# One change to a graph-attention front end on one Trainium2 core: source-term row spread ahead of the branch, first head's bounds spread by TensorE, out-degrees tied into the attention, edge test behind the first counts

## The chip, the cores and the metric

The kernel runs on one core of one Trainium2 chip. The metric is device time in microseconds; of a kernel measured several times the median counts. The kernel before took 3251.81, 3253.80 and 3253.83 us in three runs, median 3253.8.

Names of the engines: PE is TensorE's matmul stream and PEld its weight loads, DVE is VectorE, ACT ScalarE, POOL GpSimd, SP SyncE. DMAs are issued by SP and by POOL here.

## The reference

A chain of four residual stages on 1250 nodes of 1024 features with 20,000 directed edges, sorted by destination:

```python
x = x + gat(layernorm(x), W, a_l, a_r, src, dst)      # 4 heads of 256
x = x + rail_ffn(layernorm(x), ...)                    # 16384 hidden, GELU, dense way down
x = x + gcn(layernorm(x), edges, W, b)                 # degree-normalized sums
x = x + moe(layernorm(x), ...)                         # top 1 of 8 GEGLU experts, and a shared one
```

The change lies in the first stage and in one input of the third:

```python
z  = einsum('ni,hif->nhf', h, W)
el = einsum('nhf,hf->nh', z, a_l);  er = einsum('nhf,hf->nh', z, a_r)
e  = leaky_relu(el[src] + er[dst], 0.2)
ex = exp(e - segment_max(e, dst)[dst])
alpha = ex / segment_sum(ex, dst)[dst]
out = segment_sum(alpha * z[src], dst)                 # GAT
deg = 1 + (number of edges that leave a node)          # GCN uses deg ** -0.5
```

## The kernel before

Nodes are worked in T = 10 tiles of R = 125, edges in EC = 160 chunks of 125. The edge lists aren't followed one by one: the kernel builds the dense matrix of edge counts, destination by source, and does the attention densely with the counts as weights.

**Counts.** The edge lists are turned onto partitions as `ef`. For each chunk DVE makes a one-hot of the sources (`os`, 1250 wide) and one of the destinations (`od`, one or two tiles wide), and TensorE multiplies them into `pc`. `count(d)` does so for the chunks in which destination tile d can occur, given that the list is sorted and roughly even (`win[d]`, 19 chunks for the first tile); `finish` copies the counts, writes them to DRAM (`cnt_d`), writes a mask `nm` (0 where there is an edge, -1e30 elsewhere) to `nm_d`, and keeps the transposed counts in `CT` (int16, on chip). An edge test (`lim`, `out_of`, `bad`, `pf`, `flag`, lines 169 to 185) finds out whether any edge lies outside the chunks assumed for it. If so, a branch (`tc.If(elsewhere > 0)`, line 251) counts again over all chunks. With these inputs it isn't taken, but every engine waits at it and meets the others after it.

**Projections.** `z_tile(g, t)` multiplies the normalized nodes of tile t with the weights of heads 2g and 2g+1, copies the product to `Z` (ACT), and DVE forms `el` and `er` for these two heads by four dots (`sc`, line 143). The first pair of heads is projected between the counts, the second after the branch.

**Maxima and bounds.** `el` of two heads is turned into a row, written to DRAM (`to_row`: a TensorE transpose, a copy `st` on ACT, a DMA of POOL) and broadcast from there to 125 partitions (`spread`: another DMA of POOL) as `els`. `maxima(g)` then reads `nm` back tile by tile and takes the maximum of `nm + els` for each destination and head (line 271). It is advanced three steps per `z_tile`. From the maxima `bounds(g)` makes, per head, two values for each destination (`bd`), turns them into a row and spreads it likewise: `rr`, of 2 x 1250 per partition. These rows carry the head's destination term and stabilizer for every partition of the attention.

**Attention.** `attend(h, b)` does head h for half b of the destinations. For each of the ten source tiles s: DVE forms `u` from the row `rr` and per-source terms (line 316), ACT takes the exponential (317), DVE multiplies with the counts (`w`, 320), and TensorE does five matmuls of `w` with `Z` (322), whose last column of ones gives the denominators. At the end DVE divides and adds into `X`, the residual (327 to 330). `u` and `w` have three buffers. The order is attend(0,0), (0,1), (1,0), `bounds(1)`, (1,1), (2,0), (3,0), (2,1), (3,1). The maxima of heads 2 and 3 run between the steps of (0,1) and (1,0). The out-degrees `dis` are ten row sums of `CT` on DVE, then a square root and a reciprocal; they are written beside attend(1,1) but depend on nothing there.

**Order.** A planner puts the instructions of each engine into an order of its own between such constraints; the order in the source is not the order on the engine. `tc.issue_after(x)` makes the planner place an instruction behind x. A pool's memory is handed to the next pool when its last readers are done, and the first writer there waits for them.

Of the kernel before, what the change touches and what calls it, by code (L numbers as in the profile page):

```python
# [8 lines left out]
F32 = mybir.dt.float32  # L9
# [10 lines left out]
P = 128  # L20
# [17 lines left out]
def gnn_ffn_kernel(ctx, tc, x, src, dst, gat_w, a_l, a_r, maker, up, cproj,  # L38
# [64 lines left out]
    nc.gpsimd.memset(Z[:, :, :, F:F + 1], 1.0)  # L103
    el, er, mx, el2, el8 = (zp.tile([R, H, T], F32, name=n) for n in ("el", "er", "mx", "el2", "el8"))
    xT = xTp.tile([P, KD, N], F32, name="xT")

    def to_row(pool, psp, cols, k, n):

# [5 lines left out]
        nc.gpsimd.dma_start(row, st)  # L114
        return row

    def el_row(g, pool, psp):
        return to_row(pool, psp, el[:, 2 * g:2 * g + 2, :].rearrange("p h t -> p (h t)"), 2 * T, f"el{g}")

    def spread(dst_t, row):  # L120

        nc.gpsimd.dma_start(dst_t, row.rearrange("k r -> (k r)").partition_broadcast(R))

    with tc.tile_pool(name="gw", bufs=1) as gwp, tc.tile_pool(name="gps", bufs=3, space=PSUM) as psp:
        W, aw = {}, {}
# [20 lines left out]
        with tc.tile_pool(name="cc", bufs=1) as ccp, tc.tile_pool(name="cw", bufs=2) as cwp:  # L146
# [10 lines left out]
            with tc.tile_pool(name="ce", bufs=1) as cep:  # L157
                ei = cep.tile([EC // 2, 2, 2, EP], I32, name="ei")
                for i, e in enumerate((src, dst)):
                    nc.sync.dma_start(ei[:, i], e.rearrange("(a c p) -> c a p", c=EC // 2, p=EP))  # L160
                eif = cep.tile([EC // 2, 2, 2, EP], F32, name="eif")
                nc.vector.tensor_copy(eif, ei)
                pe = psp.tile([EP, 2, EC], F32, name="pt")
                for i in range(2):
                    for g in range(2):
                        nc.tensor.transpose(pe[:, i, g * EC // 2:(g + 1) * EC // 2], eif[:, i, g, :],
                                            ident[:EC // 2, :EC // 2])
                nc.vector.tensor_copy(ef, pe)
                lim = cep.tile([EP, 2, EC], F32, name="lim")
                c0 = 0  # L170
                for c in range(1, EC + 1):
                    if c == EC or near[c] != near[c0]:
                        nc.gpsimd.memset(lim[:, 0, c0:c], float(near[c0][0] * R))
                        nc.gpsimd.memset(lim[:, 1, c0:c], float((near[c0][-1] + 1) * R))
                        c0 = c
                out_of = cep.tile([EP, 2, EC], F32, name="out_of")
                nc.vector.tensor_tensor(out_of[:, 0], ef[:, 1], lim[:, 0], op=ALU.is_lt)
                nc.vector.tensor_tensor(out_of[:, 1], ef[:, 1], lim[:, 1], op=ALU.is_ge)
                bad = cep.tile([EP, 1], F32, name="bad")
                nc.vector.tensor_reduce(bad, out_of.rearrange("p a c -> p (a c)"), AX.X, ALU.add)  # L180
                ones_col = cep.tile([EP, 1], F32, name="ones_col")
                nc.gpsimd.memset(ones_col, 1.0)
                pf = psp.tile([1, 1], F32, name="pt")
                nc.tensor.matmul(pf, bad, ones_col, start=True, stop=True)
                nc.vector.tensor_scalar(flag, pf, 0.0, None, op0=ALU.is_gt)

            def src_hot(pool, c, bufs):
                os = pool.tile([EP, N], F16, name="os", bufs=bufs)
                nc.vector.tensor_scalar(os, iota, ef[:, 0, c:c + 1], None, op0=ALU.is_equal)
# [23 lines left out]
            with tc.tile_pool(name="hot", bufs=1) as hotp, tc.tile_pool(name="gl", bufs=2) as lnp:  # L213
                hot, norm = {}, {}

                def count(d):
                    pc = psp.tile([R, 3, 512], F32, name="pc", bufs=1)
                    for c in win[d]:
                        if c not in hot:
                            hot[c] = src_hot(hotp, c, 9), dst_hot(hotp, c, near[c], 9)  # L220
                        os, od = hot[c]
                        for b, (n0, nn) in enumerate(NCH):
                            nc.tensor.matmul(pc[:, b, :nn], od[:, d - near[c][0], :], os[:, n0:n0 + nn],  # L223
                                             start=(c == win[d][0]), stop=(c == win[d][-1]))
                    finish(d, pc)

                xt = {}

                def load_x(t):
                    xt[t] = lnp.tile([R, D], F32, name="xt", bufs=4)  # L230
                    dma(nc.sync, xt[t], x_t[t])

                for t in range(4):
                    load_x(t)
                z_weights(0)
                count(0)
                for t in range(T):
                    normalize(norm, lnp, t, xt[t], xt[t])
                    turn(xT, norm, psp, t, 3)
                    z_tile(0, t)  # L240
                    if t + 4 < T:
                        load_x(t + 4)
                    if t % 2:
                        count((t + 1) // 2)
                z_weights(1)
                for d in range(T // 2 + 1, T):
                    count(d)
            row0 = el_row(0, cwp, psp)

            elsewhere = nc.values_load(flag[0:1, 0:1], min_val=0, max_val=1)  # L250
            with tc.If(elsewhere > 0):  # L251
# [7 lines left out]
                                                 start=(c == 0), stop=(c == EC - 1))  # L259
                        finish(d, pc)  # L260

        def maxima(g, mxp, row):

            els = mxp.tile([R, 2, N], F32, name="els")
            spread(els.rearrange("p a n -> p (a n)"), row)
            for d in range(T):
                nm = mxp.tile([R, N], F32, name="nm2", bufs=3 - g)
                dma(nc.sync, nm, nm_d[d])
                for h in (2 * g, 2 * g + 1):
                    sc = mxp.tile([R, N], F32, name="sc2")  # L270
                    nc.vector.tensor_tensor_reduce(sc, nm, els[:, h - 2 * g, :], scale=1.0, scalar=-3.0e38,  # L271
                                                   op0=ALU.add, op1=ALU.max, accum_out=mx[:, h, d:d + 1])
                    yield

        def bounds(g, pool, psp, rowp):

            hs = slice(2 * g, 2 * g + 2)
            for dst_t, f in ((el2, SLOPE), (el8, 1.0 - SLOPE)):
                nc.vector.tensor_scalar(dst_t[:, hs], el[:, hs], f, None, op0=ALU.mult)
            top = pool.tile([R, 2, T], F32, name="top")  # L280
            nc.vector.tensor_tensor(top, mx[:, hs], er[:, hs], op=ALU.add)
            nc.vector.scalar_tensor_tensor(top, top, SLOPE, top, op0=ALU.mult, op1=ALU.max)
            bd = pool.tile([R, 2, 2, T], F32, name="bd")
            nc.vector.tensor_tensor(bd[:, :, 0], er[:, hs], top, op=ALU.subtract)
            nc.vector.scalar_tensor_tensor(bd[:, :, 1], er[:, hs], SLOPE, top, op0=ALU.mult, op1=ALU.subtract)
            for h in range(2):
                rows[2 * g + h] = rowp.tile([R, 2, N], F32, name="rr", bufs=2)
                spread(rows[2 * g + h].rearrange("p a n -> p (a n)"),
                       to_row(pool, psp, bd[:, h].rearrange("p a t -> p (a t)"), 2 * T, f"bd{2 * g + h}"))

# [1 line left out]
        rowst = ExitStack()  # L292
        rowp = rowst.enter_context(tc.tile_pool(name="rowp", bufs=1, side="right"))
        with tc.tile_pool(name="mx0", bufs=1) as mxp:
            search = maxima(0, mxp, row0)
            for t in range(T):
                for _ in range(3):
                    next(search, None)
                z_tile(1, t)
            bounds(0, mxp, psp, rowp)  # L300
# [7 lines left out]
    with tc.tile_pool(name="att", bufs=3) as atp, tc.tile_pool(name="aps", bufs=6, space=PSUM) as aps, \  # L308
            tc.tile_pool(name="tps0", bufs=2, space=PSUM) as tps:

        def attend(h, b, between=iter(())):
# [12 lines left out]
            for i in range(HT):  # L324

                rs = small.tile([R, 1], F32, name="rs")
                nc.vector.tensor_scalar(rs, po[i][:, F:F + 1], 0.5, None, op0=ALU.max)
                nc.vector.reciprocal(rs, rs)
                xs = X[:, b * HT + i, h * F:(h + 1) * F]
                nc.vector.scalar_tensor_tensor(xs, po[i][:, :F], rs, xs, op0=ALU.mult, op1=ALU.add)  # L330

        with tc.tile_pool(name="mx1", bufs=1) as mxp:
            def degrees():

                for t in range(T):
                    nc.vector.tensor_reduce(dis[:, t:t + 1], CT[:, t, :], AX.X, ALU.add)
                    if t == T - 1:
                        nc.vector.tensor_scalar(dis, dis, 1.0, None, op0=ALU.add)
                        nc.scalar.activation(dis, dis, AF.Sqrt)
                        nc.vector.reciprocal(dis, dis)  # L340
                    yield

            row1 = el_row(1, mxp, tps)
            attend(0, 0)
            search = maxima(1, mxp, row1)
            attend(0, 1, search)
            attend(1, 0, search)
            bounds(1, mxp, tps, rowp)
            attend(1, 1, degrees())
        xT = xTp.tile([P, KD, N], F32, name="xT")  # L350
        with tc.tile_pool(name="al", bufs=2) as lnp:
            attend(2, 0)
# [517 lines left out]
```

## Time and profile before

| | value |
|---|---|
| median of 3 runs | 3253.8 us |
| profiled execution | 3250.55 us, its span 3248.8 us |
| TensorE busy | 3156.3 us, 97% of the span |
| DVE / ACT / POOL busy | 51% / 11% / 4% |
| first count matmul | 12.28 us |
| branch left behind | about 246 us |
| first maximum | 261.90 us |
| TensorE's projections end | 297.99 us |
| first `u`, first matmul of the attention | 319.09 us, 322.30 us |
| last `X` of attend(1,0) | 413.33 us |

Times in the profile are microseconds from the span's start. A group of instructions is written as line, engine, operation, output<-inputs, partitions x elements, and how many; in timelines the start and the duration stand ahead of it, and a bracket behind it gives the engine's idle time just before and what ended it. The chain of waits follows the work that ended last back from the last instruction, in order of time: start, duration, what; "issue" is time for which the profile shows no cause. The windows show, per stretch, each engine's busy time with its number of instructions, then TensorE's granted clock, the DMA engines' busy share and what they moved.

### The profile page before, as it was taken

What the parts mean: (1) busy time and instruction counts of PE and PEld (TensorE: products, weight loads), DVE (VectorE), ACT (ScalarE), POOL (GpSimd) and SP (SyncE); (2) the same over time, 40 slices, a digit from 0 to 9 for tenths busy, and PEclk for the clock granted to TensorE, in tenths of its full rate; (3) what the DMA queues carried; (4) which work ended last, traced back from release to release, by engine and by line L of the source; (5) the groups of instructions that cost most, each with busy time, mean ns of one, the idle gap of its engine ahead of it and who ended that gap; (6) DMA issues with size and microseconds to landing.
All of it is one profiled execution on the core that took longest, in us unless ns stands there. A gap on an engine that the chain in (4) does not pass through costs nothing.

```text
span 3248.8 us, 23843 instructions
## 1 busy us (share of the span) xinstructions
PE 3156.3 (97%) x9330; PEld 1550.1 (48%) x9330; DVE 1642.0 (51%) x2621; ACT 354.8 (11%) x470; POOL 140.7 (4%) x222
## 2 busy tenths in 40 slices
PE   8997898999999999999999999999999899999998
PEld 5573685444444444444444444444444344445774
DVE  6567997555555555555555545555555811111113
ACT  1211234001000000100000010001000011000000
POOL 1000000000000000000000000000000000001001
PEclk9998999999999999999999999999999999999999
DMA  4245511101101110110111011101100201213564
GB/s 116 60 111 138 143 32 62 33 28 39 40 27 33 40 33 27 40 40 27 34 34 39 27 33 40 33 27 40 39 26 13 81 0 47 63 41 104 187 209 153
DMA packets 105021, 189.76 MB, mean 58 GB/s; under 512 B 32773, under 2 KB 51305, under 8 KB 104148
## 3 DMA queue, kind: packets, MB, share of 16 engines
q1 hardware_dynamic: 93618, 156.14, 16.0%
q0 software_dynamic: 11280, 31.97, 3.6%
q8 instruction: 78, 1.28, 0.2%
q14 instruction: 45, 0.37, 0.0%
HBM read 156.86 MB, written 31.21 MB: 58 GB/s over the span
## 4 chain that ended last, share of the span: by engine, by line
PE 85%; DVE 3%; issue 2%; DMA 1%; ACT 0%; POOL 0%; DVEq 0%; POOLq 0%; SPq 0%; ACTq 0%
PE po L493 59%; PE pab L674 5%; PE ph L643 5%; PE ph L583 4%; PE po L322 4%; PE pz L445 3%; PE po L778 2%; PE pt L90 1%; PE po L789 1%; DVE sc L271 1%; PE pg L629 1%; DVE w L320 0%; DVE u L316 0%; DVE st L76 0%; DVE y L781 0%
## 5 line engine op out<-in xcount | busy, mean ns | idle before, releaser
L493 PE MATMUL po<-B,gt 128*125 128x512 f32 x1920 | 836.3, 593 | 0.0
L498 DVE TENSOR_TENSOR acc<-po,acc 125x512 f32<-125x512 f32 x620 | 425.6, 689 | 486.4 <-PE po L493 483.2
L493 PEld LDWEIGHTS po<-B,gt 128*125 128x125 f32 x1920 | 360.7, 188 | 464.7 <-issue 456.8
L493 PE MATMUL po<-t,s 128*125 128x512 f32 x1280 | 559.8, 592 | 0.0
L493 PEld LDWEIGHTS po<-t,s 128*125 128x125 f32 x1280 | 237.9, 188 | 294.0 <-issue 293.6
L504 DVE TENSOR_TENSOR X<-po,X 125x512 f32<-125x512 f32 x320 | 220.7, 690 | 262.4 <-PE po L493 262.4
L493 PE MATMUL po<-B,s 128*125 128x512 f32 x640 | 299.5, 607 | 0.0
L493 PE MATMUL po<-t,gt 128*125 128x512 f32 x640 | 280.4, 593 | 2.8 <-DVE X L502 2.3
L447 ACT ACTIVATE gt<-pz 128x1668 f32<-128x1668 f32 (+1 forms) x96 | 149.8, 1560 | 688.6 <-PE pz L445 688.6
L322 PE MATMUL po<-Z,w 125*125 125x257 f32 x800 | 186.6, 394 | 24.7 <-DVE w L320 21.1
L493 PEld LDWEIGHTS po<-t,gt 128*125 128x125 f32 x640 | 120.0, 188 | 157.9 <-issue 145.8
L493 PEld LDWEIGHTS po<-B,s 128*125 128x125 f32 x640 | 112.5, 187 | 165.3 <-issue 108.9
L322 PEld LDWEIGHTS po<-Z,w 125*125 125x125 f32 x800 | 152.6, 194 | 57.2 <-DVE w L320 24.0
L643 PE MATMUL ph<-Hs,cs 125*125 125x512 f32 x400 | 173.5, 593 | 0.0
L502 DVE TENSOR_TENSOR X<-X,po 125x512 f32<-125x512 f32 x160 | 109.4, 685 | 120.2 <-PE po L493 120.2
L138 PE MATMUL pz<-W,xT 128*125 128x512 f32 x320 | 141.2, 596 | 0.2 <-PEq L251 0.2
L583 PE MATMUL ph<-W,xT 128*125 128x512 f32 x320 | 140.2, 597 | 0.0
L436 ACT COPY pw<-pz 128x128 f32<-128x128 f32 x32 | 8.5, 265 | 1131.4 <-PE pz L433 1131.4
L223 PE MATMUL pc<-os,od 125*125 125x417 f16 (+1 forms) x642 | 120.1, 345 | 1.0 <-DVE od L194 1.0
L643 PEld LDWEIGHTS ph<-Hs,cs 125*125 125x125 f32 x400 | 74.4, 188 | 93.0 <-issue 93.0
L674 PE MATMUL pab<-xgT,w 128*128 128x256 f32 x512 | 112.0, 380 | 1.4 <-DVE xgT L771 1.4
L674 PEld LDWEIGHTS pab<-xgT,w 128*128 128x128 f32 x512 | 96.7, 190 | 15.5 <-DVE xgT L771 1.9
(183 smaller groups left out, 2109.9 us busy)
## 6 DMA issues: line engine op xcount, KB each, us to landing
B<-in_cproj SPq DMA_DIRECT2D x128, 512.0 KB, 3.9
w<-in_w SPq DMA_DIRECT2D x16, 1024.0 KB, 7.0
nm<-nm_d SPq DMA_DIRECT2D x20, 546.9 KB, 4.4
w3t<-in_w SPq DMA_DIRECT2D x8, 1024.0 KB, 7.3
ys_d<-y SPq DMA_DIRECT2D x16, 512.0 KB, 5.4
cnt_d<-cn SPq DMA_DIRECT2D x10, 546.9 KB, 6.0
nm_d<-nm SPq DMA_DIRECT2D x10, 546.9 KB, 6.6
cs<-cnt_d SPq DMA_DIRECT2D x10, 546.9 KB, 4.4
```

What stands on the lines that cost most here:

```text
L138: nc.tensor.matmul(pz, xT[:, k, t * R:(t + 1) * R], W[g][:, k], start=(k == 0), stop=(k == KD - 1))
L223: nc.tensor.matmul(pc[:, b, :nn], od[:, d - near[c][0], :], os[:, n0:n0 + nn], start=(c == win[d][0]), stop=(c == win[d][-1]))
L322: nc.tensor.matmul(po[i], w[:, i * R:(i + 1) * R], Z[:, s, h, :], start=(s == 0), stop=(s == T - 1))
L445: nc.tensor.matmul(pz[:, q, :nn], pw[b][rows, :], xT[rows, b % KD, n0:n0 + nn], start=True, stop=True)
L447: nc.scalar.activation(gt[b][:, :, n0:n0 + nn], pz[:, :, :nn], AF.Gelu)
L493: nc.tensor.matmul(po, a[:, k, n * R:(n + 1) * R], w[:, k, :], start=(k == 0), stop=(k == 1))
L498: tt(acc[m][:, n, :], po, acc[m][:, n, :], op=ALU.add)
L502: tt(x, x, po, op=ALU.subtract)
L504: tt(x, po, x, op=ALU.add)
L583: nc.tensor.matmul(ph[:, g, :], xT[:, k, t * R:(t + 1) * R], W[:, k, g * 512:(g + 1) * 512], start=(k == 0), stop=(k == KD - 1))
L643: nc.tensor.matmul(pa[:, g, :], cs[:, c, :], Hs[:, c, g * 512:(g + 1) * 512], start=(c == late_first[0]), stop=(c == late_first[-1]))
L674: nc.tensor.matmul(pab[:, :nn], w12[:, i, k, f * P:(f + 1) * P], rhs[:, k, n0:n0 + nn], start=(k == 0), stop=(k == KD - 1))
```

## The change

It has four parts.

1. The edge test is moved behind `count(0)`; its tiles move to a pool that lives longer.
2. `els` is spread in front of the branch, right behind its row; it gets a pool of its own (`elp`), and `maxima` is given it. For heads 2 and 3 row and broadcast stand together likewise.
3. `bounds`: the row of the first head doesn't go through DRAM. TensorE transposes each of its 20 columns, broadcast along the free axis, so that every partition gets the 125 values; the six PSUM tiles are copied to `rr` by ACT (four) and DVE (two). The other heads' rows are made as before.
4. The ten row sums of `dis` are each tied behind the last `X` operation of attend(1,0).

```diff
-    def el_row(g, pool, psp):
-        return to_row(pool, psp, el[:, 2 * g:2 * g + 2, :].rearrange("p h t -> p (h t)"), 2 * T, f"el{g}")
...
+    def el_rows(g, pool, psp):
+        els = elp.tile([R, 2, N], F32, name="els")
+        spread(els.rearrange("p a n -> p (a n)"),
+               to_row(pool, psp, el[:, 2 * g:2 * g + 2, :].rearrange("p h t -> p (h t)"), 2 * T, f"el{g}"))
+        return els
...
-                lim = cep.tile([EP, 2, EC], F32, name="lim")
...
-                nc.vector.tensor_scalar(flag, pf, 0.0, None, op0=ALU.is_gt)
...
                 count(0)
+                lim = ccp.tile([EP, 2, EC], F32, name="lim")
...
+                        nc.gpsimd.memset(lim[:, 0, c0:c], float(near[c0][0] * R))
+                        nc.gpsimd.memset(lim[:, 1, c0:c], float((near[c0][-1] + 1) * R))
...
+                nc.vector.tensor_tensor(out_of[:, 0], ef[:, 1], lim[:, 0], op=ALU.is_lt)
+                nc.vector.tensor_tensor(out_of[:, 1], ef[:, 1], lim[:, 1], op=ALU.is_ge)
...
+                nc.vector.tensor_reduce(bad, out_of.rearrange("p a c -> p (a c)"), AX.X, ALU.add)
...
+                nc.tensor.matmul(pf, bad, ones_col, start=True, stop=True)
+                nc.vector.tensor_scalar(flag, pf, 0.0, None, op0=ALU.is_gt)
...
-            row0 = el_row(0, cwp, psp)
+            els0 = el_rows(0, cwp, psp)
             elsewhere = nc.values_load(flag[0:1, 0:1], min_val=0, max_val=1)
...
-        def maxima(g, mxp, row):
-            els = mxp.tile([R, 2, N], F32, name="els")
-            spread(els.rearrange("p a n -> p (a n)"), row)
+        def maxima(g, mxp, els):
...
                 rows[2 * g + h] = rowp.tile([R, 2, N], F32, name="rr", bufs=2)
+                if 2 * g + h == 0:
+                    for i in range(2):
+                        for t0 in range(0, T, 4):
+                            n = min(4, T - t0)
+                            pb = psp.tile([P, 4, R], F32, name="pt")
+                            for t in range(n):
+                                nc.tensor.transpose(pb[:R, t, :], bd[:, h, i, t0 + t:t0 + t + 1].to_broadcast([R, R]),
+                                                    ident[:R, :R])
+                            copy = nc.vector.tensor_copy if t0 == 4 else nc.scalar.copy
+                            copy(rows[0][:, i, t0 * R:(t0 + n) * R], pb[:R, :n, :].rearrange("p a b -> p (a b)"))
+                    continue
...
-            def degrees():
+            def degrees(after):
                 for t in range(T):
-                    nc.vector.tensor_reduce(dis[:, t:t + 1], CT[:, t, :], AX.X, ALU.add)
+                    with tc.issue_after(after.ins):
+                        nc.vector.tensor_reduce(dis[:, t:t + 1], CT[:, t, :], AX.X, ALU.add)
...
-            attend(1, 0, search)
+            end = attend(1, 0, search)
             bounds(1, mxp, tps, rowp)
-            attend(1, 1, degrees())
+            attend(1, 1, degrees(end))
```

More of the change, by code (lines that the diff above doesn't have):

```diff
@@ L105, in gnn_ffn_kernel @@
     xT = xTp.tile([P, KD, N], F32, name="xT")
+    elp = gat.enter_context(tc.tile_pool(name="elp", bufs=1, side="right"))
     def to_row(pool, psp, cols, k, n):
@@ L168, in gnn_ffn_kernel @@
                 nc.vector.tensor_copy(ef, pe)
-                lim = cep.tile([EP, 2, EC], F32, name="lim")
[L170 to L184, printed above, removed]
-                nc.vector.tensor_scalar(flag, pf, 0.0, None, op0=ALU.is_gt)
             def src_hot(pool, c, bufs):
@@ L236, in gnn_ffn_kernel @@
                 count(0)
+                lim = ccp.tile([EP, 2, EC], F32, name="lim")
+                c0 = 0
+                for c in range(1, EC + 1):
+                    if c == EC or near[c] != near[c0]:
+                        nc.gpsimd.memset(lim[:, 0, c0:c], float(near[c0][0] * R))
+                        nc.gpsimd.memset(lim[:, 1, c0:c], float((near[c0][-1] + 1) * R))
+                        c0 = c
+                out_of = ccp.tile([EP, 2, EC], F32, name="out_of")
+                nc.vector.tensor_tensor(out_of[:, 0], ef[:, 1], lim[:, 0], op=ALU.is_lt)
+                nc.vector.tensor_tensor(out_of[:, 1], ef[:, 1], lim[:, 1], op=ALU.is_ge)
+                bad = ccp.tile([EP, 1], F32, name="bad")
+                nc.vector.tensor_reduce(bad, out_of.rearrange("p a c -> p (a c)"), AX.X, ALU.add)
+                ones_col = ccp.tile([EP, 1], F32, name="ones_col")
+                nc.gpsimd.memset(ones_col, 1.0)
+                pf = psp.tile([1, 1], F32, name="pt")
+                nc.tensor.matmul(pf, bad, ones_col, start=True, stop=True)
+                nc.vector.tensor_scalar(flag, pf, 0.0, None, op0=ALU.is_gt)
                 for t in range(T):
@@ L294, in gnn_ffn_kernel @@
         with tc.tile_pool(name="mx0", bufs=1) as mxp:
-            search = maxima(0, mxp, row0)
+            search = maxima(0, mxp, els0)
             for t in range(T):
@@ L329, in attend @@
                 xs = X[:, b * HT + i, h * F:(h + 1) * F]
-                nc.vector.scalar_tensor_tensor(xs, po[i][:, :F], rs, xs, op0=ALU.mult, op1=ALU.add)
+                end = nc.vector.scalar_tensor_tensor(xs, po[i][:, :F], rs, xs, op0=ALU.mult, op1=ALU.add)
+            return end
         with tc.tile_pool(name="mx1", bufs=1) as mxp:
-            def degrees():
+            def degrees(after):
                 for t in range(T):
-                    nc.vector.tensor_reduce(dis[:, t:t + 1], CT[:, t, :], AX.X, ALU.add)
+                    with tc.issue_after(after.ins):
+                        nc.vector.tensor_reduce(dis[:, t:t + 1], CT[:, t, :], AX.X, ALU.add)
                     if t == T - 1:
@@ L341, in degrees @@
                     yield
-            row1 = el_row(1, mxp, tps)
+            els1 = el_rows(1, mxp, tps)
             attend(0, 0)
-            search = maxima(1, mxp, row1)
+            search = maxima(1, mxp, els1)
             attend(0, 1, search)
-            attend(1, 0, search)
+            end = attend(1, 0, search)
             bounds(1, mxp, tps, rowp)
-            attend(1, 1, degrees())
+            attend(1, 1, degrees(end))
         xT = xTp.tile([P, KD, N], F32, name="xT")
```

## The prediction

> **What bounds the kernel now.** I read the page's busy shares first, then its chain, then the stretch that the change touches, by chain, timeline and windows.
>
> ```profile
> PE 3156.3 (97%) x9330; PEld 1550.1 (48%) x9330; DVE 1642.0 (51%) x2621; ACT 354.8 (11%) x470; POOL 140.7 (4%) x222
> ...
> PE 85%; DVE 3%; issue 2%; DMA 1%; ACT 0%; POOL 0%; DVEq 0%; POOLq 0%; SPq 0%; ACTq 0%
> ...
> L322 PE MATMUL po<-Z,w 125*125 125x257 f32 x800 | 186.6, 394 | 24.7 <-DVE w L320 21.1
> ```
>
> TensorE is the bound: some 93 us without it in the span, and the third line puts 24.7 us of these before the attention's matmuls. The 51% of DVE is an average over stages and says nothing of one. The chain of waits, around that gap:
>
> ```profile
> 248.45 0.53 POOL els L122
> 248.98 59.90 issue
> ...
> 308.90 0.51 POOL rowbd L114
> 309.40 1.34 issue
> ...
> 310.76 0.50 POOL rr L122
> ...
> 311.28 7.67 DMA rowbd<-st
> ...
> 319.09 2.43 DVE u L316 x3
> 321.52 0.73 DVE w L320
> ...
> 322.30 36.17 PE po L322 x150
> ```
>
> A row goes to DRAM at 308.90, its broadcast is issued at 310.76 and lands at about 319, and only then the first `u` and the first matmul come. The timeline shows how the maxima ahead of it got so late:
>
> ```profile
> 246.25 16.97 PE L138 MATMUL pz<-W,xT 128*125 128x512 f32 x39 [0.15 <-PEq L251]
> ...
> 247.81 5.54 DVE L336 TENSOR_REDUCE dis<-CT 125x1 f32<-125x1250 int16 x4 [3.02 <-DVEq L251]
> ...
> 248.44 0.53 POOL L122 DMA_DIRECT2D els<-rowel  x1 [13.82 <-DVEq L251]
> ...
> 261.90 1.46 DVE L271 CUSTOM_DVE_ANT_0 sc<-nm,els 125x1250 f32<-125x1250 f32 x1 [8.20 <-DMA nm<-nm_d]
> ```
>
> The source row waits on POOL for the branch (13.82 us), is sent beside the `nm` loads, and the first maximum runs 15 us after the branch. The bracket names `nm`, whose loads were the later event by the records; `els`, issued at 248.44, is the other input. From 261.9 DVE works without a gap. TensorE's second Z group ends at 297.99: nothing of maxima or bounds is on the path before that time, everything after it is. Windows of the gap (PE, PEld, DVE, ACT, POOL busy, clock, DMA share, GB/s):
>
> ```profile
> 298.00:300.00 2.00, 0.00 (x0) 0.00 (x0) 2.00 (x5) 0.00 (x0) 0.00 (x0) 1.00 0.00 0
> 302.00:320.00 18.00, 0.96 (x3) 0.22 (x3) 8.42 (x28) 2.38 (x6) 2.58 (x5) 0.50 0.31 71
> ```
>
> And where the degrees go, attend(1,1), DVE's timeline:
>
> ```profile
> 413.33 0.47 DVE L330 SCALAR_TENSOR_TENSOR X<-po,rs,X 125x256 f32<-125x256 f32 x1
> 413.73 1.51 DVE L320 SCALAR_TENSOR_TENSOR w<-u,CT 125x625 f32<-125x625 f32 x2
> ...
> 430.12 0.81 DVE L320 SCALAR_TENSOR_TENSOR w<-u,CT 125x625 f32<-125x625 f32 x1 [0.45 <-PE po L322]
> ```
>
> The last line is DVE's first wait for TensorE: between 413.73 and 430 DVE has no idle time for anything new.
>
> **What the Trainium skill says.** "TensorE: Matmul & The Clock Gate", Part 1, What's actually happening: about 3.4 us idle halves the clock, about 3.4 us of work restores it. The trace agrees: idle from 298.0, clock 0.50 from 302, matmuls from 322.3, full again by 330. "VectorE: DVE Perf Modes", The perf-mode tier table: `tensor_reduce` has only the 1x mode; here 1250 int16 take 1448 ns, so they are dear. "DMA: Bandwidth & Descriptors", Anatomy of one DMA: about 2.0 us fixed. Agrees: the small row waits 1.87 us (308.89 to 310.76). "ScalarE: Activation LUTs", What ACT_TABLE_LOAD costs: 1283 ns and a drain of about 1380; the trace shows 1.28 us at 319.00, and no drain between it and the exponential at 320.30.
>
> **The change, part by part.** *1. Edge test behind count(0).* DVE's first `os` moves from 11.48 to where `out_of` starts, 9.20: 2.28 us earlier. The test's DVE work (0.31+0.32+0.47+0.13 busy) is paid after the 19 one-hot pairs, while TensorE works on counts; its 36 memsets on POOL go behind the W loads, one matmul goes behind count(0)'s transposes, and SP's flag load behind loads which nothing awaits before the branch. The counts run at DVE's pace there (a pair 0.62, its matmuls 57 in 12.99), so part of the lead is given back when the test comes: I take 1.9 us of lead for all that follows, because TensorE is then busy 18.5 to 20 of every 20 us. Ends: 0.5 and 2.3. TensorE ends its Z group at **E = 296.1**.
>
> *2. Source row ahead of the branch.* The row is written at 234.11 in the trace; its broadcast can be issued 2 to 5 us after and lands 8 to 12.6 us later (what the two broadcasts take here), so at about the branch. With `nm` loads alone 4.4 us, the first maximum comes at about 251, 11 us earlier; 20 maxima at 1.38 and the Z dots between them end near 288, before E. Behind the broadcast on POOL stand only its own flag load and branch, reached by about 240 in place of 234, still ahead of the join at 246. The maxima leave the path; TensorE's Z group then sets it, so the earliness beyond E is worth nothing.
>
> *3. First head's bounds by TensorE.* Bounds are ready before E, but in the changed PE order the 20 transposes stand behind the last Z tile. From E: Z copy 0.6 (`0.57 ACT L139`), four dots of 0.35 on DVE (1.4), then the copies. 20 transposes are not seen in this form; the nearest, 125x125 ones, are about 0.15 us warm and 0.23 cold, 3 to 4.6 in all, overlapping the copies (ACT 500 columns 0.58, 250 columns 0.37, DVE about 0.69). The last copy, the small row of head 1 (0.25 on ACT) and its POOL issue are at E+4.65. The first `u` of the changed program still waits for that small row, since its pool takes over the row's staging tile: 1.8 us. POOL loses the first row's write and broadcast (0.5 each); its next ones, head 1's broadcast and the X loads, follow as before. So `u` starts at E+6.5 = 302.6 in place of 319.09: **-16.5**, the lead in it. Ends: -18 with no DMA wait, and -11 if the small row lands as late as the 4.6 us of `rowel`, with transposes and copies in series (+2.5).
>
> *4. Degrees in attend(1,1).* Ten reduces, pitch 1.37 (13.7). Let T0 be the end of the last `X` of attend(1,0), 413.73 before; TensorE has then two `w` in hand, to 414.6. Changed DVE order: two reduces, `w3`, reduce, `w4`, then reduce, `u`, `w` to `w10`. That is 10 x 1.37 + 8 x 0.72 + 6 x 0.78 = 24.1 us to `w10`, and a steady step of 2.87 against TensorE's 2.17. After `w10` come three `u`, first ends of the sums, a BN statistic and `w1` of attend(2,0), 5 us more: TensorE starts attend(2,0) at T0+29.3. Before, it ran without a gap: 410.24 + 10 x 2.17 = 431.9 = T0+18.2. **+11.1**, not recovered, since attention is then TensorE's. Ends: 8 (the five ends overlap) to 13.7 (all of it). Two more table loads and the square root (2.8 on ACT) run beside `u` and the ends; ends 0 and +1.5.
>
> *5. Clock.* TensorE idles some 2.6 us before `w3` and 2.9 before attend(2,0). In the trace idle times of 2.6 us at about 400 were followed by half clock. The cold start at 322.3 cost about 2.9 us (the matmuls to 328.2 at half speed); I take 0.4 of one: **+1.2**, ends 0 and 6. The cold start itself stays, at 305.8.
>
> Sum: -16.5 + 11.1 + 1.2 = **-4.2**. The profiled execution is 3250.55 (span 3248.8), so 3246.3; it lies 3.25 below the median of 3253.8, hence 3249.6 for the median. About 0.2%, 6.5 us, is what a measurement of this kernel can tell from no change.
>
> **Rivals.** *A, the reduces hide.* `u` and `w` take 1.50 of every 2.17 us, so 6.7 us of ten steps are free, and three `w` buffers may cover two steps, 4.3. Then only 13.7 - 11.0, about 2.7, is paid, without a cold clock: -13.8, **3240**. For it: the same wait of 0.45 in every later step. Against: no wait at all from 413.73 to 430.
>
> *B, the clock falls again and again (slower).* A DVE-bound step leaves 0.7 us of TensorE idle in each 2.87; a half-speed TensorE catches up, warms, idles again. Each fall costs up to 2.9; -16.5 + 11.1 = -5.4 is passed at the second, and -5.4 + 5 x 2.9 = +9.1 with five, **3263**; over 0.2% from the fifth on. For it: clock 0.5 at 372 to 380 and 400 to 403, in a stage that DVE binds. Against: only two falls there in 50 us, and at half speed a step is longer than DVE's, which ends the idling.
>
> *C, it does half of what it says.* If `els` still lands late (its 12.6 us beside other loads) or the first lead is lost, the maxima end on DVE a few us past E, the gain is about 12, and the degrees take it: 0, **3253.8**.
>
> **How the numbers follow.** Chances: my forecast 0.55, own range -9 to +1; A 0.22; C 0.11; B 0.12. A quarter of the forecast passes -6.5, so faster 0.14 + 0.22 = 0.36; within 0.41 + 0.11 = 0.52; slower 0.12. Range 3240 to 3259: it cuts half of A, two thirds of B and some tail, about 0.2.
>
> **What would show it.** First `os` near 9.2 and Z ending near 296; `els` issued before the branch and first maximum near 251; no `dis` among the maxima; first `u` near 302.6, first attention matmul near 305.8, the wait before it a small row's. In attend(1,1) waits of TensorE for `w` of some 8 us in sum and DVE solid for 29 us; attend(2,0) only 5 us earlier than before. I am wrong if TensorE runs through attend(1,1) without gaps (A), if the clock row shows several falls after 395 (B), or if the first `u` waits past 310 (C).

## Result and profile after

The changed kernel took 3242.55 us (median of 12 runs, 3241.87 to 3252.81), the kernel before 3251.52 in the same series (12 runs, 3248.47 to 3254.50): ratio 0.998, 95% interval 0.9971 to 0.9989, or 6.5 us (3.6 to 9.4). The changed kernel's runs fall into two groups some 7 us apart (with the 21 further runs below, 19 of 33 at 3241.8 to 3244.2 and 14 at 3249.3 and above; those of the kernel before spread as far, without so clear a gap), and its profiled execution, 3252.81 with a span of 3251.1, is of the upper one; the cause is shown below.

The page of the changed kernel: TensorE's busy time and its attention group.

```profile
PE 3169.1 (97%) x9349; PEld 1556.9 (48%) x9349; DVE 1644.3 (51%) x2623; ACT 359.1 (11%) x475; POOL 137.8 (4%) x220
...
L335 PE MATMUL po<-Z,w 125*125 125x257 f32 x800 | 189.9, 397 | 27.0 <-DVE w L333 23.5
```

The wait for `w` is no smaller than before (21.1 us then), though the start of the attention moved by 18 us. It has changed places. The timeline of the changed kernel at the branch and at the attention's start:

```profile
236.15 0.53 POOL L120 DMA_DIRECT2D els<-rowel  x1 [4.28 <-DMA rowel<-st]
...
250.42 1.46 DVE L272 CUSTOM_DVE_ANT_0 sc<-nm,els 125x1250 f32<-125x1250 f32 x1 [1.13 <-DMA nm<-nm_d]
...
295.06 2.45 PE L296 MATMUL pt<-ident,bd 125*125 125x125 f32 x18
...
301.16 2.43 DVE L329 SCALAR_TENSOR_TENSOR u<-rr,el 125x625 f32<-125x625 f32 x3 [2.47 <-DMA rowbd<-st]
...
304.36 7.90 PE L335 MATMUL po<-Z,w 125*125 125x257 f32 x24 [4.89 <-DVE w L333]
```

`els` goes out some 7 us ahead of the branch (TensorE goes on behind it at 243.49), the first maximum comes at 250.42 in place of 261.90, the transposes stand directly behind the Z group, and the wait of the first `u` is for the small row of head 1. First `u` 301.16 in place of 319.09, first matmul 304.36 in place of 322.30. And TensorE alone in attend(1,1), the same trace (start, duration, in brackets the idle time before):

```profile
391.76 4.57 PE L335 MATMUL po<-Z,w 125*125 125x257 f32 x20 [0.99 <-DVE w L333]
398.82 4.60 PE L335 MATMUL po<-Z,w 125*125 125x257 f32 x20 [2.49 <-DVE w L333]
405.12 2.43 PE L335 MATMUL po<-Z,w 125*125 125x257 f32 x10 [1.71 <-DVE w L333]
407.98 2.43 PE L335 MATMUL po<-Z,w 125*125 125x257 f32 x10 [0.43 <-DVE w L333]
...
419.43 2.43 PE L335 MATMUL po<-Z,w 125*125 125x257 f32 x10 [0.43 <-DVE w L333]
424.58 55.59 PE L335 MATMUL po<-Z,w 125*125 125x257 f32 x245 [2.71 <-DVE w L333]
```

Where the kernel before ran without a gap, every step now ends in one: 2.49 and 1.71 at the head, 0.43 in each step of 2.86 us, 2.71 ahead of attend(2,0). So 10.6 of the 17.9 us are given back by 424.58, where attend(2,0) starts 7.3 us earlier than before (431.9).

### The profile page after: what moved, and what is told of

The parts are those of the page before. It is cut to its first block, busy times and chain, and to the rows that moved or that the text cites. A ratio compares the mean times of both kernels' runs of the same rounds, so it can differ in the third digit from the quotient of the medians.

```text
span 3251.1 us, 23868 instructions
## 1 busy us (share of the span) xinstructions
PE 3169.1 (97%) x9349; PEld 1556.9 (48%) x9349; DVE 1644.3 (51%) x2623; ACT 359.1 (11%) x475; POOL 137.8 (4%) x220
## 4 chain that ended last, share of the span: by engine, by line
PE 85%; DVE 4%; issue 2%; DMA 1%; ACT 0%; SPq 0%; DVEq 0%; POOL 0%; POOLq 0%; ACTq 0%
PE po L508 59%; PE pab L689 5%; PE ph L658 5%; PE ph L598 4%; PE po L335 3%; PE pz L460 3%; PE po L793 2%; PE pt L90 1%; PE po L804 1%; DVE sc L272 1%; DVE w L333 1%; PE pg L644 1%; DVE u L329 1%; DVE dis L351 0%; PE pt L784 0%
## 5 line engine op out<-in xcount | busy, mean ns | idle before, releaser
L209 PEld LDWEIGHTS <-od 125*125 125x125 f16 x642 | 88.5, 139 | 34.4 <-issue 7.9
```

## Experiments

Times are medians; the kernel before, in the same series, lay between 3250.7 and 3251.6. Where a first `u` is given, it is read from that kernel's timeline.

### The changed kernel again

No edit.

> The changed kernel once more beside the two others. Theory: median 3242 to 3246, ratio to the kernel before 0.997 to 0.998; in its profile the first u near 301.5, attend(2,0) starting 120.2 us after the first attention matmul; and, if its time is near 3242, the clock back at 1.00 within about 5 us of TensorE's restart at the FFN, in place of 25 us.

Median 3244.13 of 21 runs, ratio 0.9986 (0.9978 to 0.9994). Its profiled execution took 3242.34, and up to the attention's end it is the same as the first within 0.6 us: first `u` 300.88, attend(2,0) at 424.03. What differs comes next, at the start of the rail-FFN. TensorE's timeline and a window (PE, PEld, DVE, ACT, POOL busy, clock, DMA share, GB/s) in the first profile of the changed kernel:

```profile
526.73 3.66 PE L90 MATMUL pt<-ident,xn 125*128 125x125 f32 x16 [6.24 <-DVE rstd L81]
...
567.54 8.75 PE L508 MATMUL po<-t,gt 128*125 128x512 f32 x20
...
530.00:542.00 12.00, 11.48 (x36) 6.65 (x35) 4.41 (x10) 4.87 (x11) 2.23 (x6) 0.50 0.43 144
```

and in the second:

```profile
526.20 3.67 PE L90 MATMUL pt<-ident,xn 125*128 125x125 f32 x16 [6.24 <-DVE rstd L81]
...
560.41 8.75 PE L508 MATMUL po<-t,gt 128*125 128x512 f32 x20
...
530.00:542.00 12.00, 8.56 (x44) 4.62 (x45) 7.62 (x10) 8.61 (x13) 3.84 (x6) 0.93 0.39 127
```

The same program starts again within 0.5 us of the same time, after the same idle 6.24 us that halve the clock; in one execution the clock is back at 530.4, in the other at 551.7. By the first dense stretch of the FFN that is 7.1 us, 6.6 of them made there. The executions end 10.5 us apart; 1.7 more arise at four matmuls near 2570 (3.67 us in place of 1.98, the clock again) and 1.1 at the next start, near 2600 (32 matmuls in 15.02 us in place of 13.91). The kernel before, profiled, had the clock back at about 537. This is the main difference between the two groups of runs, and it isn't the change's doing.

### Row sums not tied

```diff
-                    with tc.issue_after(after.ins):
-                        nc.vector.tensor_reduce(dis[:, t:t + 1], CT[:, t, :], AX.X, ALU.add)
+                    nc.vector.tensor_reduce(dis[:, t:t + 1], CT[:, t, :], AX.X, ALU.add)
```

> The changed kernel with the ten row sums of dis not tied any more: the planner puts them among the maxima again (four ahead of the first maximum, two between bd and the rest). Theory (the tie costs what it was priced at): first u at about 302.4 in place of 301.16, since two row sums and the square root now stand ahead of the last copies of the first head's row; attend(1,1) without gaps, attend(2,0) starting about 112 us after the first attention matmul, where the changed kernel took 120.2; so about 9 to 10 us faster than the changed kernel, 3232 to 3234 us. Rival A (the sums hide in the attention): no difference in the attention, and 1 us slower than the changed kernel, 3243. Rival D (the maxima stage needs the room that they took): first u near 309, and as slow as the changed kernel.

3233.84, ratio 0.9947 (0.9934 to 0.9960): about 9 us better than the changed kernel, by the medians. Its timeline, DVE and TensorE:

```profile
294.68 2.82 DVE L350 TENSOR_REDUCE dis<-CT 125x1 f32<-125x1250 int16 x2
...
304.14 2.43 DVE L329 SCALAR_TENSOR_TENSOR u<-rr,el 125x625 f32<-125x625 f32 x3 [2.66 <-DMA rowbd<-st]
...
395.12 50.19 PE L335 MATMUL po<-Z,w 125*125 125x257 f32 x227 [0.99 <-DVE w L333]
```

Two of the sums stand behind `bd` again and the first `u` is 3.0 us later (1.2 were expected), but attend(1,1) and what follows is one stretch. The tie's balance is thus shown: 3 us gained ahead, about 11 lost in attend(1,1).

### The tie alone, on the kernel before

The same four lines as in the change, without the other edits.

> The kernel before with the fourth edit alone (row sums tied behind the last X of attend(1,0)). Theory: six row sums leave DVE between 261.9 and 307.5, of which about 7 us count after TensorE's Z group ends, so the first u comes near 312 in place of 319.1; attend(1,1) then costs 11 us more; 3254 to 3257 us, slower than the kernel before by 3 to 5 us. Rival A (sums hide in the attention): 3244 to 3246, faster by 6. Rival D: no gain ahead, 11 us slower, 3262.

3252.37, ratio 1.0006 (0.9998 to 1.0015): the first `u` came at 310.59, 8.5 us earlier, and attend(1,1) cost its 11 us. The expectation was 2 us too slow because it took the gain for 7. Where DVE is the maxima stage's last engine, taking six sums away is worth 8.5; where the other edits have taken it off the end, only 3. In the kernel before, four of the six stand among maxima and dots, and the last two hold the row up by another way, in its timeline:

```profile
304.67 2.81 DVE L336 TENSOR_REDUCE dis<-CT 125x1 f32<-125x1250 int16 x2
...
307.73 0.21 ACT L339 ACTIVATE dis<-dis 125x10 f32<-125x10 f32 x1 [15.98 <-DVE dis L338]
```

`bd` is ready at 304.67, but on ACT the square root of `dis` stands ahead of the row's copy `st`, which therefore comes only at 308.35.

### First head's row by way of DRAM

```diff
-                if 2 * g + h == 0:
-                    ...
-                    continue
```

> The changed kernel with the first head's row by way of DRAM again (third edit undone). Theory: staging copy at about 295.8, row written and waited for 1.9 us, broadcast 8 us: first u near 306.3 in place of 301.16, so 5 us slower than the changed kernel, 3247 to 3248. Rival (the prediction's split, in which the third edit carried all of the 16.5): first u near 317 and 3257. Rival (the transfer is hidden): first u near 301, 3242.

3250.19, ratio 1.0000 (0.9992 to 1.0008): without this edit nothing measurable is left of the gain. Its first `u`:

```profile
307.35 2.43 DVE L317 SCALAR_TENSOR_TENSOR u<-rr,el 125x625 f32<-125x625 f32 x3 [9.21 <-DMA rowbd<-st]
```

6.2 us later than in the changed kernel, 0.6 of which it was already late at its first `os` (9.96 against 9.34): 5.6 us for the third edit.

### els behind the branch, two attempts

The first moved the call behind `tc.If` in the source and left the pool `elp`:

```diff
-            els0 = el_rows(0, cwp, psp)
+            row0 = el_row(0, cwp, psp)
...
-            search = maxima(0, mxp, els0)
+            search = maxima(0, mxp, el_spread(row0))
```

> The changed kernel with els broadcast behind the branch again (second edit undone). Theory: issue near 246, landing beside the nm loads near 259, first maximum near 259 in place of 250.4; the maxima then end on DVE near 298, after TensorE's Z group (295.1), and the first u comes near 304 to 305: 3 us slower than the changed kernel, 3245 to 3246. Rival C (els lands late in both): no difference, 3242. Rival (it is what carries the gain): first u past 309, 3250.

3245.83, ratio 0.9983 (0.9976 to 0.9990), and not the experiment it was meant to be: POOL's timeline has the broadcast where it was.

```profile
237.28 0.53 POOL L120 DMA_DIRECT2D els<-rowel  x1 [4.51 <-DMA rowel<-st]
```

The planner put the broadcast ahead of the branch from either place in the source, its tile having memory of its own. What held it back in the kernel before should then be the tile's pool, opened behind the branch. The second attempt makes `els` a tile of the maxima's pool again:

```diff
+            els = mxp.tile([R, 2, N], F32, name="els")
+            spread(els.rearrange("p a n -> p (a n)"), row)
```

> The changed kernel with els a tile of the maxima's own pool again (as before the change), so that its broadcast can't be placed ahead of the branch; on POOL it stands behind the branch now. Theory: issue near 246.5, landing beside the nm loads near 259; first maximum near 259 to 260 in place of 250.4; the maxima and dots then end on DVE near 299, behind TensorE's Z group (295), and the first u comes near 305: 3 to 4 us slower than the changed kernel, 3246. Rival C (els lands late in any case): first u within 0.5 us of 301.2. Rival (the second edit carries most of the gain): first u past 309, 3250 and more.

3245.52, ratio 0.9985 (0.9977 to 0.9994). Its timeline, first and last maximum and first `u`:

```profile
259.06 1.46 DVE L271 CUSTOM_DVE_ANT_0 sc<-nm,els 125x1250 f32<-125x1250 f32 x1 [9.22 <-DMA nm<-nm_d]
...
293.44 1.46 DVE L271 CUSTOM_DVE_ANT_0 sc<-nm,els 125x1250 f32<-125x1250 f32 x1
...
301.76 2.43 DVE L328 SCALAR_TENSOR_TENSOR u<-rr,el 125x625 f32<-125x625 f32 x3 [2.02 <-DMA rowbd<-st]
```

The broadcast is issued behind the branch again, at 246.16, so it is the pool that decides. The maxima start 8.6 us later and end 7 to 8 us later, at 294.9, just ahead of the Z group's end (295.7); the first `u` is as early as in the changed kernel (its first `os` was 0.55 late). My sum of 3 to 4 us was wrong because it put all dots of the Z tiles ahead of the last maximum; DVE had room for the 20 maxima in the 36 us from 259. With the row sums gone from this stage, the second edit brings nothing. Whether it brings something with the sums in it, as in the untied version, was not run.

### Edge test ahead of the first counts

The block `lim` to `flag` back in its old place, its tiles too.

> The changed kernel with the edge test ahead of the first counts again (first edit undone). Theory: first os near 11.5 in place of 9.3, TensorE's Z group ends near 297.3 to 298 in place of 295.1, first u near 303.5 to 304: 2 to 3 us slower than the changed kernel, 3245. Rival (the lead is swallowed by waits between the counts): Z group ends at 295 to 296 all the same, 3242.5.

3245.21, ratio 0.9984 (0.9975 to 0.9993); first `os` 11.49, Z group ending at 297.8 in place of 295.2, first `u` 303.71: 2.55 us for the first edit in this pair of profiles.

The pair doesn't stand for all. In the ten profiles with the edit the first `os` starts between 9.07 and 10.26, since DVE has the statistics of the first tiles of `x` ahead of it and waits for their load (2.86 us in the first profile of the changed kernel, 2.44 in the second); in the three without, it starts at 11.48 or 11.49. In all ten the Z group ends 285.7 to 285.8 us behind the first `os`, here 286.1. So the edit is worth 1.6 to 2.8 us, 2.3 on average.

### Row sums on ACT

```diff
+                cd = mxp.tile([R, N], F16, name="cd")
+                nc.scalar.activation(cd, CT[:, t, :], AF.Identity, accum_out=dis[:, t:t + 1])
```

in the loop over `z_tile(1, t)`, with the sum's end ahead of `bounds(0)`; none left on DVE.

> The changed kernel with the ten row sums on ACT (an identity activation over CT that accumulates, one each about 1.3 us) in the maxima stage, none on DVE. Theory (what the degrees cost is DVE time in the attention, and ACT has room in the maxima stage): first u near 301.2 as in the changed kernel, attend(1,1) without gaps, attend(2,0) at about 112.5 us after the first attention matmul; 3 us faster than the untied version (3233.8), so 3230.5 to 3231.5. Rival (what helped in the untied version was that the loads or the clock fell better): no faster than 3234.

3231.32, ratio 0.9940 (0.9927 to 0.9953), the best of all, as expected: 19 us under the kernel before, 11 under the changed one. The group and TensorE's timeline in the attention:

```profile
L314 ACT ACTIVATE cd<-CT 125x1250 f16<-125x1250 int16 x10 | 12.5, 1246 | 6.2 <-DVEq L254 6.0
...
391.51 53.66 PE L340 MATMUL po<-Z,w 125*125 125x257 f32 x243 [1.00 <-DVE w L338]
```

The sums are no dearer on ACT (1.25 us and 0.19 for reading the accumulator); there they delay the first two Z copies, which nothing waits for. First `u` 300.85 and no gap in attend(1,1).

### Row sums thin, over attend(2,0) and attend(3,0)

Each sum tied behind the latest `w`, one behind every second step.

> The changed kernel with the ten row sums still on DVE, but one behind every second step of attend(2,0) and attend(3,0) in place of one a step in attend(1,1). Theory (the sums cost what DVE lacks in the step where they stand: 2 x 1.50 + 1.37 = 4.37 for two steps, against TensorE's 4.34): attend(1,1) without gaps and almost none in the two that follow, up to 3 us lost; 3232 to 3235. Rival (ten sums on DVE cost their 11 us wherever they stand in the attention): 3242 as the changed kernel.

3237.93, ratio 0.9962 (0.9949 to 0.9974): better than the tie in attend(1,1), worse than expected. TensorE's timeline:

```profile
438.79 10.79 PE L337 MATMUL po<-Z,w 125*125 125x257 f32 x46 [0.69 <-DVE X L345]
450.51 11.53 PE L337 MATMUL po<-Z,w 125*125 125x257 f32 x52 [0.94 <-DVE w L335]
...
473.02 2.43 PE L337 MATMUL po<-Z,w 125*125 125x257 f32 x10 [1.01 <-DVE w L335]
```

Small gaps, until TensorE restarts at the FFN at 520.94, 6.9 us behind the ACT version (514.04). The sum 4.37 against 4.34 had left out what else DVE does there: ten ends of sums (`X`, 0.40 each) and the BN statistics. The cost of a sum depends on the room in its steps, between nothing and 1.1 us, and neither the theory's figure nor the rival's holds.

### Keeping TensorE at work ahead of the FFN

```diff
+            pt = tps.tile([P, 4, R], F32, name="pt")
+            for k in range(9):
+                nc.tensor.matmul(pt.rearrange("p a b -> p (a b)"), ident, xT[:, k % 5, :4 * R], start=(k == 0), stop=(k == 8))
```

behind the last `attend`; it adds work whose result isn't used.

> The changed kernel with nine more matmuls (128x500 from data at hand, their result used by nothing) behind the attention's last, in the 6.24 us in which TensorE waits for the next norm. Theory (the clock's fall in this gap and its late return cost 3 us in some runs and about 10 in others): the clock row stays at 1.00 from 520 to 543, the FFN's first dense stretch starts some 2.5 us earlier than in the better runs of the changed kernel, all runs lie together near 3240, none near 3250. Rival (the slower runs have another cause): still two groups some 8 us apart, at 3242 and 3250.

3242.27 with all seven runs at 3241.96 to 3244.13, ratio 0.9972 (0.9961 to 0.9983): the upper group is gone (with 14 of 33 in it, seven runs would miss it by chance in 2 of 100 cases). The time of the lower one is not improved, since the nine matmuls outlast the gap:

```profile
520.59 7.71 PE L393 MATMUL pt<-xT,ident 128*128 128x500 f32 x18
```

With seven of them, on the ACT version:

> Degrees on ACT in the maxima stage together with seven unused 128x500 matmuls (nine took 7.7 us and outlasted the 6.24 us gap; seven should take 6.0) behind the attention's last. Theory (the two effects are separate and add): runs in one group near 3229 to 3230, 1.5 us below the ACT version alone (3231.3) and without its odd slower run (3238.1). Rival (the warm-up work costs what it saves, as with nine): 3231 to 3232, but in one group.

3234.66, ratio 0.9949 (0.9936 to 0.9962): 3.3 us worse than without by the medians of five runs each, though the intervals overlap. The matmuls end within the gap and the transposes start 0.9 us earlier, but then TensorE waits 1.90 us for a norm, and the clock falls there:

```profile
517.00:519.00 2.00, 1.51 (x11) 1.35 (x12) 1.23 (x4) 0.84 (x4) 0.44 (x2) 1.00 1.05 386
519.00:521.00 2.00, 2.00 (x6) 0.88 (x6) 0.98 (x2) 0.69 (x3) 0.00 (x0) 0.52 0.92 302
```

It stays at half until 536. So the clock at this place is the cause of the upper group: with the nine it stayed at 1.00 through it, and the group vanished. The mean granted clock of each run says the same, 0.990 or 0.991 in the 14 and 0.993 or 0.994 in the 19; a difference of 0.003 over 3245 us is, as an estimate, some 20 us at half clock, and the clock came back 21 us apart in the two profiles. No remedy was found; why the clock falls with the seven and not with the nine stays open, since the two kernels differ in more than the number of matmuls.

## Why the prediction was right, point by point

| step | predicted | measured |
|---|---|---|
| lead at the end of the Z group | -1.9 (ends 0.5, 2.3) | -2.8; by undoing the edit 2.55; 1.6 to 2.8 over the profiles |
| first maximum | 251 | 250.42 |
| first `u` | 302.6, -16.5 | 301.16, -17.9 |
| end of the Z group to the first `u` | 6.5 | 5.9 |
| last `X` of attend(1,0) to the end of `w10` | 24.1 | 24.1 (395.24 to 419.30) |
| the same to attend(2,0) | 29.3, +11.1 | 29.3 (to 424.58) |
| start of attend(2,0) against before | -5.4 | -7.3 |
| clock behind it | +1.2 | +1.0 |
| TensorE's restart at the FFN against before | -4.2 | -6.3 (526.73; 533.00) |
| whole kernel | -4.2 | -6.5 by the ratio (3.6 to 9.4) |

The mechanism held as the steps have it: the first row's trip through DRAM and the row sums leave the path ahead of the attention, and the sums come back in a stage where DVE has no room. The line that carried this was DVE's first wait at 430.12 in the timeline of before; the 51% of DVE on the page would have led to rival A, which the gaps of attend(1,1) rule out. Rival B is ruled out too: the clock stayed at 1.00 from 398 to 424 in spite of a gap in each step, and fell once, behind the gap of 2.71 us. Two windows of the changed kernel (columns as above):

```profile
415.00:420.00 5.00, 4.14 (x19) 2.95 (x18) 5.00 (x7) 2.66 (x4) 0.52 (x1) 1.00 0.24 74
...
425.00:430.00 5.00, 5.00 (x17) 4.03 (x16) 5.00 (x10) 1.64 (x2) 0.00 (x0) 0.66 0.01 3
```

Rival C's first half, `els` late, was brought about in the second attempt above, and cost nothing: its step that the maxima then end on DVE a few us past E, the end of the Z group, was wrong.

Some terms were off. The 1.9 for the lead of the first edit lies within the 1.6 to 2.8 of the profiles, but the way there was another: the start was not fixed at 9.20 but waits for the load of `x`, and the lead grew on the way. Against the kernel with the test in its old place it is 2.15 at the first count matmul (10.14 and 12.29), 1.81 where count(0)'s transposes start (23.85 and 25.66), and 2.58 at count(1)'s (53.76 and 56.34), where TensorE waits 0.60 for the copy `cn` in place of 1.45. (The 36 memsets of `lim` are 38; nothing hangs on it.)

The 16.5 of part 3 were right in sum within 1.4 us, 0.9 of it the lead and 0.5 the way from there to the first `u`, but put down to the wrong edits: by undoing each, TensorE's spread is worth 5.6 at the first `u`, the edge test 2.55, `els` nothing, and the departure of the sums from the maxima 3.0 with the rest in place and 8.5 alone. The prediction named the sums as a cost only, though they also stood ahead of the first row. These figures add up to 11.2 of the 17.9: what is left belongs to several edits together. Early `els` and the departure of the sums both take DVE off the end of the stage; no run takes both back at once, so how they share the rest is open.

The clock at the FFN's start was not in the prediction at all. It moves single runs by as much as the change does, and how many runs of either kernel it catches decides the whole-kernel figure: the medians are 9.0 apart, the ratio of the first series says 6.5, that of the second, of the same two kernels, 4.6. That 6.5 lies so near the 6.3 at TensorE's restart is luck in part. In absolute terms the forecast was less good: 3249.6 was given for the median and 3242.55 measured; 2.3 of the 7 us are the kernel before, which came out at 3251.5 in place of 3253.8, the rest the terms above and this clock.

## What to carry to other kernels

A reduction moved between engines' idle times costs what the engine lacks in the very steps where it lands: the same ten sums cost 11 us, 7 us, 3 us or nothing, by place and engine, and only a timeline of that stage tells which. Look first for an engine with nothing due, here ACT. And undo edits of a bundle one by one: with the other three in place, one of the four here was worth nothing and one cost more than it brought, and the version without that one is 9 us faster than the bundle. But single undoings need not add up to the whole, as here: two edits that relieve the same engine can hide each other.

## What the runs showed of the hardware

The clock's return was less regular than I had taken it to be. "TensorE: Matmul & The Clock Gate", Part 1 of the Trainium skill, gives about 3.4 us of work to full clock, and calls the count of cold matmuls variable between runs. At the FFN's start TensorE worked 11.48 of 12 us (transposes and matmuls of 32 rows) at clock 0.50 throughout in one execution of the changed kernel, and was at full clock 4 us after the same start in another. The same part has a window of that length, running on its own, decide; as an estimate, this would shift the return by about one such window, 3.4 us, and not by the 21 us seen. No run here shows what does decide.

Nor does the clock fall only behind idle times of 3.4 us, the figure that the prediction took from there: it fell behind gaps of 1.83, 2.22 and 2.71 us. The length of the last gap alone doesn't settle it either. In the first profile of the changed kernel a gap of 2.22 us ahead of 369.26 left the clock at 1.00, and one of 1.83 us ahead of 376.40 was followed by 0.50 from 377.8; in the second, 2.22 us ahead of 368.72 was followed by 0.50 from 370.0, and 2.61 us ahead of 380.90 left it at 1.00.
